# The last experts of a two-layer model: first tiles beside the attention's last batch, gathers queued one part later, sums counted sooner

## The chip, the core and the metric

The kernel runs on one core of one Trainium2 chip. A core has several engines, each with its own queue of instructions that it executes in order: PE (TensorE: matrix products and transposes; its weight loads are shown as PEld), DVE (VectorE), ACT (ScalarE), POOL (GpSimd) and SP (SyncE, which here only issues DMAs). Engines wait for one another by semaphores. Between its inputs and outputs in HBM and the engines lie the on-chip memories SBUF and PSUM; matrix products are written to PSUM. Transfers run on 16 DMA engines.

The metric is the device time of one execution in microseconds (us), as a median of several runs. A profile is one execution taken by the hardware profiler; its span is the time from its first to its last instruction.

## What is computed

Four batches of 1024 rows with 256 columns pass two layers. Each layer has an attention and a feed-forward part with experts, both behind a modulated layer norm. The change touches only the end of the second layer, which the reference computes like this:

```python
def _L1_attn_ref(x, w_qkv, w_proj, b_proj, w_dwc, b_dwc):
    ...
    q = _norm_last(q ** FOCUS)
    k = _norm_last(k ** FOCUS)
    kv = jnp.einsum('bhnd,bhne->bhde', k, v)
    z = 1.0 / (jnp.einsum('bhnd,bhd->bhn', q, k.sum(axis=2)) + EPS)
    out = jnp.einsum('bhnd,bhde,bhn->bhne', q, kv, z)
    ...
    out = out + conv
    return jnp.einsum('bnc,oc->bno', out, w_proj) + b_proj

def _L1_ffn_ref(x, router_w, router_b, expert_w, expert_b):
    ...
    probs = jax.nn.softmax(logits, axis=-1)
    gate = jnp.max(probs, axis=-1)
    idx = jnp.argmax(probs, axis=-1)
    out_all = jnp.einsum('th,ehd->ted', xt, expert_w) + expert_b[None, :, :]
    e_out = jnp.take_along_axis(out_all, idx[:, None, None], axis=1)[:, 0, :]
    y = gate[:, None] * e_out
    ...
    x = x + ga * _L1_attn_ref(h, ...)
    h = _layernorm(x, axis=-1) * (1 + cb) + sb
    x = x + gb * _L1_ffn_ref(h, ...)
```

Every row goes to one of eight experts, the one with the greatest probability; the expert is one product with a 256 x 256 matrix.

## The kernel before

The kernel computes only the chosen expert of a row. So the rows are sorted by expert first, and every tile of 128 sorted rows belongs to one expert.

**The second attention** (`attention1`) goes over the batches with two generators: `front(b)` makes the keys, values and queries of batch b, `back(b - 1)` the output of the batch before. In the last turn of the loop (b = 4) only `back(3)` runs: ps_o (product with kv), its transposes ps_oT, the convolution y (one ACT step at L1597 and two DVE steps at L1601 for each half of the channels) and the projection ps_pr (L1609), which is added to x.

**Around it** runs other work. `k.around` (class `Around`) holds `tasks`, generators that are advanced by so many pieces after each step of the attention, and `riders`, generators of DMAs on POOL's queue, of which one instruction is issued for each "ride". A step has one ride in the attention and two in the last stage. A scatter or a gather also waits for the matmul that was the last to be emitted before it (`paced`, with `k.anchor`). Within what the dependencies allow, the order on an engine is that of a scheduler; `k.pin` keeps an instruction in the order of the program.

**The last experts** (`Experts1`) work in three parts, `PARTS = ((0, 1), (2,), (3,))`: part 0 is batches 0 and 1 (22 tiles, worked on as 11 pairs), parts 1 and 2 are one batch each (14 tiles, 7 pairs). A part goes through these steps:
- `rows(b)`, a task: the statistics of the rows, the normalised rows h (ACT, L1030; first four tiles, later the other four), their store to rows_in, transposes ps_lnT, the router's products ps_route and the logits.
- `sort(p)`, a task: a chain of small DVE operations with three small products (ps_rank, ps_expert) that gives the place of each row (index) and each tile's expert (offset).
- `send(p)`, a rider: POOL loads rows (hs, L1870) and scatters them to their sorted places (L964), 16 scatters for part 0 and 8 for each other part.
- the pairs, in `run`: SP loads a pair of tiles xs (L1008; up to four pairs ahead, and only once the part is sent), PE transposes it (ps_xT, L1923), ACT copies it to xT (L1927, or two scaled copies at L1930 in parts 1 and 2), PE multiplies it with the expert's weights (ps_y, L1938, whose addresses come from registers that each pair loads from offset, L955), DVE adds the bias (L1944) and in parts 1 and 2 multiplies by a gate (L1946), and SP stores the results.
- `combine(p)`, a task: POOL gathers the results in the order of the rows (L974), four tiles ahead of their use with six buffers ys; ACT and DVE scale them and add them to x (L2002, L2007, L2008 in part 0, L1996 in the others), and SP stores the output.

`run` begins when the attention has ended. combine(0) is put among the tasks when the last pair of part 0 is out, so it runs beside part 1's pairs, and combine(1) beside part 2's.

**A check** counts that sums of the attentions lie within bounds (`count_sums`: three times four DVE operations on 512 columns, L495 to L498, at the end of part 1) and branches at the end to a second, general computation, which does not run with these data (`out_of_bounds`).

Of the kernel before, what the change touches and what calls it, by code (L numbers as in the profile page):

```python
# [8 lines left out]
F32 = mybir.dt.float32  # L9
I32 = mybir.dt.int32  # L10
AF = mybir.ActivationFunctionType
# [54 lines left out]
def bcast(ap, axis, n):  # L66

    shape = list(ap.shape)
    shape.insert(axis, n)
    return ap.unsqueeze(axis).to_broadcast(shape)  # L70
# [430 lines left out]
def count_sums(k, pool):  # L501

    recs = [k.recs.rearrange("p n i j -> p (n i j)")]
    recs += [k.recs1[:, i].rearrange("p b t h -> p (b t h)") for i in range(2)]
    inverse = 1.0 / SUM_HI, 1.0 / SUM_LO
    for i, (rec, (low, high)) in enumerate(zip(recs, (inverse, (SUM_LO, SUM_HI), inverse))):
        good = pool.tile([P, 8 * B * H], F32, tag="xs", name="good", bufs=6)
        count_within(k, good, rec, low, high, k.good[:, i : i + 1])


def out_of_bounds(k, pool, psum):
# [505 lines left out]
def routed_rows(k, work, b, statistics, scale, shift, wr, br, ne, logits, scalar):  # L1017
# [31 lines left out]
        return h  # L1049

    h = yield from normalised(0)
    for q in range(2):
        hT = work.tile([P, CC, 512], F32, tag="hT", name="hT", bufs=1)
        for cc in range(CC):
            ps = k.misc.tile([P, 512], F32, tag="m", name="ps_lnT")
            for i in range(4):
                tr = nc.tensor.transpose(  # L1057
                    ps[:, i * P : (i + 1) * P], h[:, i, cc * P : (cc + 1) * P], k.ident
                )
                if i == 0:  # L1060
                    k.pin(tr)
            if scale is None:
                nc.scalar.activation(
                    hT[:, cc], ps, AF.Identity,
                    bias=k.modF[:, cc, b : b + 1], scale=k.modF[:, 2 + cc, b : b + 1],
                )
            else:
                nc.scalar.copy(hT[:, cc], ps)
            if q == 0 and cc == CC - 1:
                h = yield from normalised(1)  # L1070
            else:
                yield 1
        yield from route_logits(k, hT, wr, br, ne, work, logits[:, 4 * q : 4 * q + 4])
# [368 lines left out]

def attention1(ctx, k, a, after_batch=lambda b: None):


    nc = k.nc
# [166 lines left out]
            yield  # L1615

    k.misc = ps_m
    for b in range(B + 1):
        while b == HB and k.awaited in k.around.tasks:
            k.around.step()  # L1620
        todo = ([front(b)] if b < B else []) + ([back(b - 1)] if b else [])
        pace = (6, 8, 6, 6, 12)[b]
        n = 0
        while todo:
            todo = [g for g in todo if next(g, k) is not k]
            n += pace
            k.around.step(n // 6)
            n %= 6
        if b:
            after_batch(b - 1)  # L1630

# [152 lines left out]
class Experts1:  # L1784


    def __init__(self, k, a, out):
# [16 lines left out]
        whole = Sorting(k, rt, E1, 1, NT * len(PARTS[0]))  # L1804
        fewer = whole.of_fewer(rt, NT)
        self.sortings = [whole if len(p) > 1 else fewer for p in PARTS]
        self.sent = set()

    def load_weights(self):
        k, a, nc = self.k, self.a, self.k.nc  # L1810
# [52 lines left out]
    def send(self, p, index):  # L1863
# [16 lines left out]
                yield  # L1880
        self.sent.add(p)

    def run(self, early):

        k = self.k
        nc = k.nc
        work = self.back = self.stack.enter_context(
            k.tc.tile_pool(name="f1_work", bufs=2, reuse_waits="tile")
        )
        ps_x = self.stack.enter_context(  # L1890
            k.tc.tile_pool(name="f1_ps_x", bufs=4, space=PSUM, reuse_waits="tile")
        )
        ps_o = self.stack.enter_context(
            k.tc.tile_pool(name="f1_ps_o", bufs=4, space=PSUM, reuse_waits="tile")
        )
        k.misc = ps_x

        pairs = [
            (p, list(range(g, min(g + 2, s.tiles))))
            for p, s in enumerate(self.sortings)  # L1900
            for g in range(0, s.tiles, 2)
        ]
        coming = []

        def fetch(n):

            for p, tiles in pairs[n + len(coming) : n + 5]:
                if p not in self.sent:
                    break
                xs = work.tile([P, 2, C], F32, tag="xs", name="xs", bufs=6)  # L1910
                k.sorted1[p].load(xs[:, : len(tiles)], tiles)
                coming.append(xs)

        def tiles_of(p, tiles, xs):

            n = len(tiles)
            at = self.sortings[p].offsets(
                self.state[p][1], tiles, [mybir.EngineType.PE, mybir.EngineType.DVE]
            )
            ps = ps_x.tile([P, 2, CC, P], F32, tag="m", name="ps_xT")  # L1920
            for j in range(n):
                for cc in range(CC):
                    nc.tensor.transpose(ps[:, j, cc], xs[:, j, cc * P : (cc + 1) * P], k.ident)  # L1923
            xT = work.tile([P, 2, CC, P], F32, tag="xT", name="xT", bufs=3)
            b = PARTS[p][0] if len(PARTS[p]) == 1 else None
            if b is None:
                nc.scalar.copy(xT[:, :n], ps[:, :n])  # L1927
            else:
                for cc in range(CC):
                    nc.scalar.activation(  # L1930
                        xT[:, :n, cc], ps[:, :n, cc], AF.Identity,
                        bias=k.modF[:, cc, b : b + 1], scale=k.modF[:, 2 + cc, b : b + 1],
                    )
            yield
            po = ps_o.tile([P, 2, C], F32, tag="o", name="ps_y")
            for j in range(n):
                for cc in range(CC):
                    k.anchor = nc.tensor.matmul(  # L1938
                        po[:, j], lhsT=xT[:, j, cc], rhs=self.we[:, cc, bass.ds(at[j], C)],
                        start=cc == 0, stop=cc == CC - 1,  # L1940
                    ).ins
            y = work.tile([P, 2, C], F32, tag="y", name="y", bufs=3)
            for j in range(n):
                nc.vector.tensor_tensor(y[:, j], po[:, j], self.be[:, bass.ds(at[j], C)], ALU.add)  # L1944
            if b is not None:
                nc.vector.tensor_tensor(y[:, :n], y[:, :n], bcast(self.gate[:, b], 1, n), ALU.mult)  # L1946
            nc.sync.dma_start(k.results1[p].part(tiles), y[:, :n])

        again, before = None, None
        for n, (p, tiles) in enumerate(pairs):  # L1950
            if p not in self.sent and before is not None:
                next(before, None)
                before = None
            while p not in self.sent:
                k.around.step(1, 2)
            fetch(n)
            now = tiles_of(p, tiles, coming.pop(0))
            next(now)
            if before is not None:
                next(before, None)  # L1960
            before = now
            if n + 1 == len(pairs) or pairs[n + 1][0] != p:
                next(before, None)
                before = None
                if early and p + 2 == len(PARTS):
                    count_sums(k, work)
                if early and p + 1 == len(PARTS):
                    again = out_of_bounds(k, work, ps_x)
                k.around.tasks.append(self.combine(p))
            k.around.step(2, 2)  # L1970
        k.around.drain()
        self.stack.close()
        return again

    def combine(self, p):
        k, work = self.k, self.back
        nc = k.nc
        index, _, part = self.state[p]
        most = self.sortings[p].nt

        def fetch(n):
            ys = work.tile([P, C], F32, tag="ys", name="ys", bufs=6)
            self.sortings[p].gather(ys, k.results1[p], index[:, 0, n : n + 1])
            return ys

        coming = []
        for n in range(4):
            coming.append(fetch(n))
            yield 0.5
        for n in range(most):  # L1990
            j = n % 2
            b, t = PARTS[p][n // NT], n % NT
            ys = coming.pop(0)
            if len(PARTS[p]) == 1:
                xs = k.x[b][:, t]
                k.pin(nc.vector.scalar_tensor_tensor(  # L1996
# [2 lines left out]
            else:  # L1999
                if j == 0:  # L2000
                    y = work.tile([P, 2, C], F32, tag="out", name="out")
                k.pin(nc.scalar.activation(y[:, j], ys, AF.Identity, scale=part[:, n : n + 1]))  # L2002
            if n + 4 < most:
                coming.append(fetch(n + 4))
            if j == 1 and len(PARTS[p]) > 1:
                xs = k.x[b][:, t - 1 : t + 1]
                nc.vector.tensor_tensor(y, y, bcast(self.gate[:, b], 1, 2), ALU.mult)  # L2007
                nc.vector.tensor_tensor(xs, xs, y, ALU.add)  # L2008
            if t % 4 == 3:
                nc.sync.dma_start(  # L2010
# [7 lines left out]
def two_layers(ctx: ExitStack, tc: tile.TileContext, a: dict, out: bass.AP):  # L2018
# [56 lines left out]
    def stages(first, second, early):  # L2075
# [22 lines left out]
        with ExitStack() as s, tc.using_default_side("right"):  # L2098
            if not early:
                with tc.tile_pool(name="f0_ps_end", bufs=2, space=PSUM, reuse_waits="tile") as k.misc:  # L2100
                    k.around.drain()
            second(s, k, a, *([after_attention1] if early else []))
        if not early:
            experts1.load_weights()
            for b in range(B):
# [81 lines left out]
```

## Time and profile before

| what | value |
|---|---|
| median of 3 runs | 1087.06 us (1085.88, 1089.72, 1087.06) |
| profiled execution, its time | 1087.63 us |
| profiled execution, span | 1085.8 us |
| mean granted PE clock | 0.955 |
| PE busy | 945.7 us (87%), 6072 instructions |
| DVE busy | 620.4 us (57%), 1987 instructions |
| ACT busy | 602.5 us (55%), 959 instructions |
| POOL busy | 336.0 us (31%), 528 instructions |

In the profile a line such as `L1938 PE MATMUL ps_y<-we,xT` names the line of the program, the engine, the operation and the tiles that it writes and reads. What stands in square brackets is the idle time of the engine before the instruction, with the work that ended last before it. "issue" means that the profile shows nothing that the engine waited for. The granted clock is a share of PE's full speed. The busy time of an engine is a mean over stages that have different limits; what a change in one stage does is read from that stage.

### The profile page before, as it was taken

Reading aid. Unit: us, or ns where it says so; the run is one execution under the profiler, and the core shown is the slowest. Engines: PE = TensorE matmul, PEld = TensorE weight load, DVE = VectorE, ACT = ScalarE, POOL = GpSimd, SP = SyncE. Lnnn points to the kernel's source line nnn. Section 1 sums busy time; section 2 is a strip of 40 time slices with the busy share of each in tenths; the row PEclk is TensorE's granted clock in tenths of the full one; section 3 lists DMA queues with packets and bytes.
Section 4 is the critical chain, followed back from the end, with each engine's and each line's share of the span. In section 5 each row is a group of like instructions: output and inputs, shape, how many; then the busy total and the mean of one; then the engine's idle time right before and its main releaser. Section 6 shows DMA issues by size and latency. Waiting matters only on the chain.

```text
span 1085.8 us, 18090 instructions
## 1 busy us (share of the span) xinstructions
PE 945.7 (87%) x6072; PEld 559.8 (52%) x6072; DVE 620.4 (57%) x1987; ACT 602.5 (55%) x959; POOL 336.0 (31%) x528
## 2 busy tenths in 40 slices
PE   4899999999999999889679989986997989858760
PEld 2434434443443434335568878874464656547550
DVE  5822235422465155413676767993899968564572
ACT  0368655765477555775555657766654745523430
POOL 2013211311232234663004615612550100553632
PEclk9999999999999999999899999998999899989875
DMA  6995000100010001552825556624223201458764
GB/s 206 358 346 179 1 1 6 40 1 1 1 64 1 1 30 54 201 215 78 317 88 170 197 177 189 196 75 144 67 65 148 88 2 39 141 170 264 240 205 130
DMA packets 97142, 132.89 MB, mean 122 GB/s; under 512 B 8536, under 2 KB 84216, under 8 KB 96528
## 3 DMA queue, kind: packets, MB, share of 16 engines
q1 hardware_dynamic: 84656, 97.27, 26.9%
q0 software_dynamic: 11776, 33.57, 9.9%
q8 instruction: 52, 0.85, 0.3%
q10 hardware_dynamic: 608, 0.79, 0.3%
q14 instruction: 50, 0.41, 0.1%
HBM read 67.85 MB, written 63.75 MB: 121 GB/s over the span
## 4 chain that ended last, share of the span: by engine, by line
PE 63%; DVE 19%; issue 5%; DMA 5%; ACT 4%; POOL 1%; SPq 1%; DVEq 0%; ACTq 0%; POOLq 0%
PE ps_s L388 13%; PE ps_av L453 12%; PE ps_qk L364 6%; PE ps_y L1312 5%; PE ps_h L1247 4%; PE ps_v L349 3%; PE ps_out L427 3%; PE ps_pr L1609 3%; PE ps_y L1938 3%; PE ps_q L1537 2%; PE ps_k L1511 2%; DVE y L1601 2%; DMA ys<-results,index 2%; PE ps_lnT L1057 1%; DVE st L1258 1%
## 5 line engine op out<-in xcount | busy, mean ns | idle before, releaser
L396 ACT ACTIVATE pT<-ps_s 128x1024 f32<-128x1024 f32 x288 | 279.3, 1022 | 169.7 <-PE ps_s L388 167.2
L399 POOL TENSOR_SCALAR_AFFINE_SELECT pT<-pT 128x256 f32<-128x256 f32 x256 | 104.2, 431 | 328.4 <-ACT pT L396 323.7
L388 PE MATMUL ps_s<-qT,kT 32*128 32x512 f32 (+3 forms) x1536 | 178.8, 523 | 0.1
L453 PE MATMUL ps_av<-pT,v 128*32 128x512 f32 (+3 forms) x1536 | 165.2, 497 | 9.4 <-DVE turned L411 5.6
L964 POOL DMA_INDIRECT sorted<-hs,index x96 | 96.2, 1002 | 144.9 <-PE ps_y L1312 73.0
L974 POOL DMA_INDIRECT ys<-results,index x96 | 102.7, 1070 | 119.0 <-DMA results<-y 43.6
L388 PEld LDWEIGHTS ps_s<-qT,kT 32*128 32x128 f32 x1536 | 74.5, 185 | 95.5 <-issue 72.8
L453 PEld LDWEIGHTS ps_av<-pT,v 128*32 128x32 f32 x1536 | 40.6, 108 | 104.0 <-issue 58.7
L1247 PE MATMUL ps_h<-w,xT 128*128 x352 | 82.1, 386 | 6.5 <-DVE mv L1259 3.8
L1312 PE MATMUL ps_y<-w,act 128*128 x352 | 83.7, 392 | 4.2 <-DVE rs_seed L84 2.8
L411 DVE STREAM_TRANSPOSE turned<-ps_av 128x512 f32<-128x512 f32 x32 | 22.8, 712 | 98.9 <-PE ps_av L453 98.6
L1312 PEld LDWEIGHTS ps_y<-w,act 128*128 128x128 f32 x352 | 67.7, 197 | 14.0 <-ACT act L1295 4.8
L1247 PEld LDWEIGHTS ps_h<-w,xT 128*128 128x128 f32 x352 | 66.2, 193 | 15.9 <-issue 4.2
L1295 ACT ACTIVATE act<-ps_hT,gain 128x128 f32<-128x128 f32 x176 | 63.6, 463 | 16.9 <-PE ps_hT L1286 16.8
L1270 ACT ACTIVATE hid<-hid,nmr,rstd 128x256 f32<-128x256 f32 x88 | 47.5, 603 | 39.4 <-DVE nmr L1263 39.2
L1511 PE MATMUL ps_k<-wqkv,hT 128*128 128x512 f32 x128 | 61.9, 603 | 3.6 <-DMA wqkv<-in_wqkv_dram 2.8
L1938 PE MATMUL ps_y<-we,xT 128*128 x200 | 53.0, 412 | 10.6 <-ACT xT L1930 8.4
L371 DVE COPY qT<-ps_qk 128x512 f32<-128x512 f32 x16 | 11.0, 688 | 81.8 <-PE ps_qk L364 81.8
L103 DVE BATCH_NORM_STATS2 ln_st<-x 128x6 f32<-128x256 f32 x128 | 49.2, 407 | 0.5
L1255 DVE TENSOR_TENSOR hid<-ps_h,b 128x256 f32<-128x256 f32 x88 | 33.9, 415 | 26.6 <-PE ps_h L1247 21.5
L1938 PEld LDWEIGHTS ps_y<-we,xT 128*128 128x128 f32 x200 | 38.2, 204 | 20.1 <-ACT xT L1930 11.6
L374 DVE TENSOR_SCALAR kT<-ps_qk,par 128x512 f32<-128x512 f32 x32 | 22.5, 745 | 37.0 <-PE ps_qk L364 37.0
(223 smaller groups left out, 1499.4 us busy)
## 6 DMA issues: line engine op xcount, KB each, us to landing
xs<-sorted SPq DMA_DIRECT2D x69, 256.0 KB, 3.8
results<-y SPq DMA_DIRECT2D x69, 256.0 KB, 3.0
sorted<-zero SPq DMA_DIRECT2D x2, 6016.0 KB, 20.1
rows_in<-h SPq DMA_DIRECT2D x16, 512.0 KB, 2.9
hs<-rows_in POOLq DMA_DIRECT2D x32, 256.0 KB, 3.5
w<-in_w_dram SPq DMA_DIRECT2D x8, 1024.0 KB, 11.3
x<-in_x_dram SPq DMA_DIRECT2D x4, 1024.0 KB, 6.5
b<-in_b_dram SPq DMA_DIRECT2D x2, 2048.0 KB
```

The lines of the kernel that those rows point to most:

```text
L364: nc.tensor.matmul(ps, lhsT=w[:, cc, g * P : (g + 1) * P], rhs=hT[:, cc, hf * 512 : (hf + 1) * 512], start=cc == 0, stop=cc == CC - 1,)
L388: k.anchor = nc.tensor.matmul(pair[hh // 2][:, hh % 2, c0 : c0 + w], lhsT=kTs[o][rows, kb * P : (kb + 1) * P], rhs=qT[rows, q1 - w : q1], ...
L396: nc.scalar.activation(pT, ps, AF.Exp, scale=1.0 / L**0.5)
L399: nc.gpsimd.affine_select(out=pT[:, :, c0 : c0 + P], in_=pT[:, :, c0 : c0 + P], compare_op=ALU.is_ge, fill=0.0, base=0, pattern=[[0, 2], [ ...
L453: nc.tensor.matmul(po[32 * hh : 32 * hh + 32, 512 - w :], lhsT=vs[b % 2][:, kb, 8 * g + 2 * hh + o, :], rhs=exps[b, g, o, u][hh // 2][:, h ...
L964: i = self.k.nc.gpsimd.indirect_dma_start(out=buffer.ap, out_offset=bass.IndirectOffsetOnAxis(ap=index, axis=0), in_=rows, in_offset=None, ...
L974: self.paced(self.k.nc.gpsimd.indirect_dma_start(out=rows, out_offset=None, in_=buffer.ap, in_offset=bass.IndirectOffsetOnAxis(ap=index, a ...
L1247: mm = nc.tensor.matmul(ph[:, j], lhsT=xTs[i // 2][:, j, cc], rhs=w1[:, cc, bass.ds(at[i + j], C)], start=cc == 0, stop=cc == CC - 1,)
L1295: o = nc.scalar.activation(act[:, j, cc], pt[:, j, cc], AF.Gelu, bias=gain[:, 1, cc, t : t + 1], scale=gain[:, 0, cc, t : t + 1],)
L1312: mm = nc.tensor.matmul(po[:, j], lhsT=acts[i // 2][:, j, cc], rhs=w2[:, cc, bass.ds(at[i + j], C)], start=cc == 0, stop=cc == CC - 1,)
L1511: k.anchor = nc.tensor.matmul(ps, lhsT=hT[:, cc, t * P : (t + 1) * P], rhs=wqkv[:, cc, C:], start=cc == 0, stop=cc == CC - 1,).ins
L1938: k.anchor = nc.tensor.matmul(po[:, j], lhsT=xT[:, j, cc], rhs=self.we[:, cc, bass.ds(at[j], C)], start=cc == 0, stop=cc == CC - 1,).ins
```

## The change

Five things are changed, all in the last 160 us:

1. `attention1` calls a function `fill(turn)` in the last turn of its loop. It is `Experts1.beside`: in turns 6, 7 and 8 it emits two, one and one of part 0's pairs. They use two tiles of the attention's pool (spare) in place of the buffers of `run`, and the attention's PSUM tiles. The code of a pair (`fetch`, `tiles_of`) moves from `run` to methods; the first transpose, the copies xT and the first product of each tile are pinned.
2. In the turns b = 3 and b = 4 of the attention a step has two rides.
3. Where the rows are not scaled (batches 2 and 3), `routed_rows` normalises all eight tiles before the first transposes.
4. The gathers become riders (`gathers(p)`), queued when the last pair of a part is out, with 24 buffers ys. combine(0) becomes a task at the end of part 1's pairs, combine(1) and combine(2) after all pairs. A step in `run` has four pieces until the last part is sent.
5. `count_sums` becomes a generator; one of its three counts is emitted after each of the pairs 7, 8 and 9 of part 0, and its tile good gets another tag. `out_of_bounds` comes after all pairs.

```diff
 def count_sums(k, pool):
...
-        good = pool.tile([P, 8 * B * H], F32, tag="xs", name="good", bufs=6)
+        good = pool.tile([P, 8 * B * H], F32, tag="out", name="good")
         count_within(k, good, rec, low, high, k.good[:, i : i + 1])
+        yield
...
     h = yield from normalised(0)
+    second = (yield from normalised(1)) if scale is None else None
...
             if q == 0 and cc == CC - 1:
-                h = yield from normalised(1)
+                if second is None:
+                    h = yield from normalised(1)
+                else:
+                    h = second
+                    yield 1
...
+    k.bank = lambda name: ps_p.tile([P, 2, C], F32, tag="p", name=name)
+    k.spare = lambda: work.tile([P, CC, N], F32, tag="hT", name="spare")
     for b in range(B + 1):
...
             n += pace
-            k.around.step(n // 6)
+            k.around.step(n // 6, 1 + b // (B - 1))
             n %= 6
+            turn += 1
+            if b == B:
+                fill(turn)
...
+    def pair(self):
+
+        self.fetch()
+        p, tiles = self.pairs[self.done]
+        self.done += 1
+        now = self.tiles_of(p, tiles, self.coming.pop(0))
+        next(now)
+        self.products()
+        self.before = now
+        if self.done == len(self.pairs) or self.pairs[self.done][0] != p:
+            self.products()
...
+    def beside(self, turn):
+
+
+        if 0 not in self.sent or turn > 8:
+            return
+        if self.space is None:
...
+            self.space, self.most = space, 4
+        self.fetch()
+        for _ in range({6: 2, 7: 1, 8: 1}.get(turn, 0)):
+            self.pair()
+        if turn == 8:
+            self.products()
...
+        counts = count_sums(k, work) if early else iter(())
+        last = len(PARTS) - 1
+        while self.done < len(self.pairs):
+            p = self.pairs[self.done][0]
+            if p not in self.sent:
+                self.products()
             while p not in self.sent:
-                k.around.step(1, 2)
...
+                around.step(1, 2)
+            self.pair()
+            if p == 0 and self.done > 6:
+                next(counts, None)
+            if self.done == len(self.pairs) or self.pairs[self.done][0] != p:
+                around.riders.append(self.gathers(p))
+                if p == last - 1:
+                    around.tasks.append(self.combine(0))
+            around.step(2 if last in self.sent else 4, 2)
+        for _ in counts:
+            pass
+        again = out_of_bounds(k, work, ps_x) if early else None
+        while around.riders:
+            around.step(0)
+        around.tasks += [self.combine(p) for p in range(1, last + 1)]
+        around.drain()
...
+    def gathers(self, p):
+
+        index = self.state[p][0]
+        for n in range(self.sortings[p].nt):
+            ys = self.back.tile([P, C], F32, tag="ys", name="ys", bufs=24)
+            self.sortings[p].gather(ys, self.k.results1[p], index[:, 0, n : n + 1])
+            self.got[p].append(ys)
+            yield
...
-            ys = coming.pop(0)
+            while not self.got[p]:
+                k.around.step(0)
+            ys = self.got[p].pop(0)
...
-            second(s, k, a, *([after_attention1] if early else []))
+            second(s, k, a, *([after_attention1, experts1.beside] if early else []))
```

## The prediction

> **What bounds the kernel now.** The change touches only the last 160 us, so I read those. First the busy time of each engine in six stretches (from:to, length, then busy us and instructions of PE, weight loads, DVE, ACT and POOL, the granted PE clock, DMA share, GB/s):
>
> ```profile
> core 0: us, PE busy (x) PEld busy (x) DVE busy (x) ACT busy (x) POOL busy (x), PEclk, DMA share, GB/s
> 945.20:960.50 15.30, 5.98 (x56) 4.83 (x56) 12.46 (x45) 6.03 (x10) 8.50 (x10) 0.78 0.47 151
> 960.50:969.50 9.00, 9.00 (x36) 7.58 (x35) 4.56 (x15) 0.00 (x0) 2.08 (x2) 0.80 0.68 219
> 969.50:1006.40 36.90, 31.57 (x198) 24.76 (x197) 17.17 (x74) 13.96 (x26) 16.80 (x19) 1.00 0.80 253
> 1006.40:1033.50 27.10, 19.20 (x82) 15.13 (x82) 15.49 (x30) 13.13 (x29) 17.71 (x17) 0.87 0.72 224
> 1033.50:1062.20 28.70, 18.97 (x78) 14.77 (x78) 22.68 (x51) 7.24 (x15) 8.47 (x8) 0.82 0.66 209
> 1062.20:1085.80 23.60, 0.00 (x0) 0.00 (x0) 3.79 (x9) 0.00 (x0) 8.07 (x8) 0.52 0.39 118
> ```
>
> The first two are the end of the second attention (convolution on ACT and DVE, then the projection ps_pr). The third holds part 0's eleven pairs of tiles and, between them, the routing and sorting of the last batch. The fourth is part 1, the fifth part 2, the sixth the last gathers and stores. In no stretch after 969.5 but the third is PE near full, so the pairs wait for something. The timeline (start, length) says for what, with the wait in square brackets:
>
> ```profile
> 956.56 0.97 POOL L964 DMA_INDIRECT sorted<-hs,index  x1 [0.30 <-issue]
> 959.07 11.75 SPq L1008 DMA_DIRECT2D xs<-sorted  x8
> 960.40 0.20 PE L949 MATMUL ps_expert<-past,all 8*1 8x14 f32 x2 [7.67 <-DVE index L933]
> 960.54 8.94 PE L1609 MATMUL ps_pr<-wg,y 128*128 128x256 f32 x32
> 1019.01 3.54 PE L1938 MATMUL ps_y<-we,xT 128*128 x8 [3.58 <-ACT xT L1930]
> 1048.90 2.30 PE L1923 MATMUL ps_xT<-ident,xs 128*128 128x128 f32 x8 [6.42 <-DMA xs<-sorted]
> 1061.46 0.69 DVE L1946 TENSOR_TENSOR y<-y,gate_f 128x512 f32<-128x512 f32 x1
> 1065.12 1.00 POOL L974 DMA_INDIRECT ys<-results,index  x1 [14.78 <-DMA results<-y]
> ```
>
> Three marks carry the sum: ps_pr ends at 960.54 + 8.94 = 969.48 (T); the first ps_y of part 1 starts at 1006.40 (S); the span ends at 1085.8, 79.4 after S. The waits from 1006.4 to 1062.2 (total, times, longest):
>
> ```profile
> ACT out L2002 <- DMA ys<-results,index: 10.6, 8, 2.6
> PE ps_y L1938 <- ACT xT L1930: 8.4, 4, 3.6
> PE ps_xT L1923 <- DMA xs<-sorted: 6.4, 1, 6.4
> ```
>
> ACT waits in its own order for a gathered tile, and the scaled copies xT stand behind it, so PE waits for ACT; later PE waits for a load of xs that stands on SP behind stores of results.
>
> **Part by part.** *Two riders a step.* From its first scatter at 927.17 POOL issues a scatter every 1.31 us and an hs load every 1.06 (the rows of L964 and L1870). In the built order 4 hs loads stand between the 16 scatters: 15 x 1.31 + 4 x 1.06 = 23.9, so the last starts at 951.1 and not 956.56: 5.5 earlier. The loads of xs follow 2.5 later (956.56 to 959.07) and land in 3.8 to 4.1: the first tile is there at 957.6 (L). If the scatters keep the waits that they have now for buffers (1.74 and 2.10 on POOL), L is nearer 960; if the loads had landed as fast as the results do (3.0), 956.6. I take 957.6, as the waits came where one rider a step held the queue.
>
> *First pairs beside the attention.* The built order on PE is what matters. The first ps_xT of a pair, which waits for all 16 scatters and the load, now stands before the rest of the last batch: three ps_o tiles, the second lnT and route of batch 2, the eight ps_oT, logits, rank, then four pairs' ps_y, ps_expert, ps_pr. Before, ps_xT stood behind ps_pr. So from about 945.5 PE does nothing until L, some 12 us, and the attention waits with it. After L:
> - the work that ran from 945.24 to 951.08 (5.8 us), mostly still to do, 5.5; at half clock for its first 3.6 us, 1.8 more: ps_oT ends at L + 7.3;
> - from ps_oT to ps_pr it took 951.08 to 960.54 = 9.5 (ACT y, then four DVE steps L1601 of 1.20). Now ACT has two copies xT between its two y (2 x 0.59), and DVE has four bias adds (0.42 and 0.34) and two to four register loads of 0.53 (the median of L955 on DVE's queue) between those steps: 1.2 + 1.5 + 1.1 to 2.1, so 3.8 to 4.8; the last step also stands behind pair 1's y, some 1 more. PE's four pairs (8 transposes of two pairs 1.04, 8 records of ps_y 1.99: 2.5 each, 10.1) fit beside that. ps_pr starts at L + 21.5 to 24; I take 22.5;
> - ps_pr without the half clock: 1.3 less than 8.94, 7.6.
>
> T becomes 957.6 + 22.5 + 7.6 = 987.7: **18.2 later**.
>
> *T to S.* Four pairs fewer stand here, 10.1 us of PE. They buy little: the stretch is a chain from ps_pr over statistics (mv at T + 4.2), normalise, transposes, route, logits (T + 18.9), the sort (index at T + 26), ps_expert, then pairs 7 to 10, counted from 0 (y from 997.41) and S. The built order still puts ps_y of pairs 7 to 10 behind ps_expert. The second normalise goes ahead, but ACT does all eight in a row before the first hT copy, so one gains what the other loses; the logits come about 0.5 earlier. Two of the counts of sums (0.42 + 0.42 + 0.68 + 0.68 by L495 to L498) now stand among the sort's small DVE steps: 0.5 to 1.5. Taken: 37.4 for 36.9, **0.5 later**; from 5 earlier (PE's idle 36.9 - 31.57 = 5.3, if it was PE that held the chain) to 1.5 later.
>
> *S to the end.* Gathers are queued on POOL one part later into 24 buffers and no ACT or DVE instruction waits for them in part 1: pairs at the rate of the undisturbed ones (ps_y at 1006.40 and 1008.70, 2.2 with the next), 7 x 2.2 = 15.4. Part 2's first load of xs is queued on SP ahead of part 1's stores of results, so the wait of 6.42 goes; but it waits for part 2's scatters, behind which those stores stand: hidden as long as it lands before S + 15.4 (last scatter about S + 3, landing about 7 more), else its lateness is added. In part 2 combine(0) runs beside the pairs, and DVE sets the rate: 7 x (0.67 + 0.6) for y and gate, 8 x (0.6 + 0.6) for out and x, 7 x 0.53 of register loads: 22.2. Then the tail as now, 1085.8 - 1062.15 = 23.65 (the gathers of part 2 wait for all its results, as before; combine(1) lies in their wait of some 3 + 10.5 us). S to end: 15.4 + 22.2 + 23.65 = 61.2 instead of 79.4: **18.2 earlier**, 14 to 20 by part 2 at 2.8 (before's 1056 to 1062) or with one more half clock stretch.
>
> Sum against the profiled run: +18.2 + 0.5 - 18.2 = +0.5; span 1086.3, and with 1.8 around it (1087.63 - 1085.8) 1088.1. The profiled run lies 0.6 above the median of 1087.06, so this is +0.5 on like terms; I keep 1088.5.
>
> The half clock speaks against this change. The rows show what idling PE costs:
>
> ```profile
> 960.40:964.00 3.60, 3.60 (x10) 2.92 (x11) 0.21 (x2) 0.00 (x0) 0.00 (x0) 0.50 0.96 294
> 1048.90:1056.10 7.20, 6.81 (x21) 5.22 (x22) 2.23 (x6) 2.04 (x4) 1.22 (x1) 0.50 0.67 234
> ```
>
> After 7.7 idle the clock is 0.50 for 3.6 us, after 6.4 idle for 7.2. The new stall of 12 us invites either: 1.8 (taken) or 3.6.
>
> The Trainium skill, "TensorE: Matmul & The Clock Gate", section "What's actually happening", has the clock fall to half after an idle window of about 3.4 us and come back after as long a busy one. The first row agrees, the second stays down twice as long; by the page the price would be 1.7 and the time 1088, by the second row 3.6 and 1090, and its advice to avoid such gaps speaks against putting a waiting transpose ahead of ready work.
>
> **Rivals.** *The chain from T to S was held by PE.* For it: PE is busy 31.57 of 36.9 there. Against it: the logits wait for ACT's h and hT, and rank for DVE. If so S comes 5.3 sooner, and the full gain behind S (20) adds 1.8: 1088.1 - 7.1 = 1081. *The first load is late.* The attention now waits for POOL's last scatter. Each us that L is late is a us of the end. For it: POOL's scatters now wait for buffers (1.74 and 2.10); with these and a lag as today's the load lands at 959.07 + 3.9 = 963, 5.4 later: 1093.5, and with the clock down 7.2 us 1095.3. It decides from L = 960 (1090.3 is 2.2 above the sum). Against it: nothing else stands on POOL then. *The riders and early pairs are hidden anyway* would give the 18.2 without the stall, 1070; the built order speaks against it, since ps_oT can't pass ps_xT on PE.
>
> **How the numbers follow.** Gain and stall cancel: 0.42, own range 1083 to 1094. PE held the chain (or a shorter stall): 0.28, 1072 to 1083. The first load late (or a slower part 2): 0.30, 1091 to 1102. The predicted time is the first's, 1088.5. A measurement of this kernel can tell 0.3% (3.3 us) from no change, so same is 1083.8 to 1090.3. Of the first case 0.04 lies below it, 0.24 in it, 0.14 above: faster 0.32, same 0.24, slower 0.44. For 8 in 10 the range runs from 1077 to 1101.
>
> **What would show it.** PE idle from about 945 to L near 957.6, ended by a DMA into spare, with ps_oT behind it; ps_pr ending at 987 to 989; 36 to 38.5 from there to part 1's first ps_y; no wait of ACT for ys before part 2; part 2's pairs 2.9 to 3.2 apart with DVE nearly full; the tail near 23.6. Wrong if the stall is under 8 us or over 16, if the early pairs shorten T to S by over 2, or if part 1 waits for its stores behind part 2's loads.

## The result and the profile after

The changed kernel took 1096.3 us (median of 5 runs, 1093.42 to 1098.08) against 1087.06 (5 runs): a ratio of 1.0081, with a 95% interval of 1.0057 to 1.0105. It is slower, by 0.8%. Its profiled execution has a span of 1095.9 us, 10.1 more than before.

The busy time by stages after the change (the columns are those of before):

```profile
core 0: us, PE busy (x) PEld busy (x) DVE busy (x) ACT busy (x) POOL busy (x), PEclk, DMA share, GB/s
946.60:961.47 14.87, 0.77 (x9) 0.54 (x5) 0.68 (x2) 0.62 (x1) 8.12 (x9) 0.59 0.49 153
961.47:989.60 28.13, 25.85 (x142) 21.58 (x143) 18.84 (x65) 7.19 (x11) 6.45 (x7) 0.85 0.43 140
989.60:1029.02 39.42, 27.55 (x152) 21.69 (x149) 20.63 (x81) 11.91 (x22) 12.86 (x15) 0.83 0.57 188
1029.02:1044.50 15.48, 15.23 (x82) 13.14 (x82) 7.71 (x16) 7.80 (x17) 9.73 (x11) 1.00 0.79 257
1044.50:1070.30 25.80, 16.33 (x78) 11.94 (x78) 22.06 (x43) 12.00 (x27) 16.75 (x16) 0.97 0.85 265
1070.30:1095.90 25.60, 0.00 (x0) 0.00 (x0) 8.26 (x19) 0.00 (x0) 8.22 (x8) 0.50 0.51 162
```

The first row is new: for 14.9 us four engines do next to nothing and only POOL works. The fourth row is the gain: part 1 on a PE that is full, 15.5 us where part 1 took 27.1. The third row took 36.9 before and has fewer pairs in it now, but a lower clock. The timeline after:

```profile
954.03 0.98 POOL L965 DMA_INDIRECT sorted<-hs,index  x1 [0.31 <-issue]
...
956.60 1.90 SPq L1009 DMA_DIRECT2D spare<-sorted  x4
...
961.47 0.48 PE L1921 MATMUL ps_xT<-ident,spare 128*128 128x128 f32 x1 [14.10 <-DMA spare<-sorted]
...
968.61 1.09 PE L1595 MATMUL ps_oT<-ident,on 128*128 128x128 f32 x8
...
982.43 7.17 PE L1615 MATMUL ps_pr<-wg,y 128*128 128x256 f32 x32
...
994.58 0.47 PE L1059 MATMUL ps_lnT<-ident,h 128*128 128x128 f32 x1 [4.54 <-ACT h L1031]
...
1074.98 1.00 POOL L975 DMA_INDIRECT ys<-results,index  x1 [9.16 <-DMA out_dram<-x]
```

PE waits 14.1 us for the first early pair's load. The last ps_o tiles and the second half of ps_oT, which PE had done by 951.1 in the kernel before, come after it. The marks of the prediction give this balance. "Start" is the first scatter of part 0, which is ahead of the stages compared here; what lies before it was 2.3 us longer in this execution. That difference is there long before anything that the change touches: ps_expert of the first layer starts at 573.92 instead of 571.98. In all fourteen profiles of this document that mark lies between 569.2 and 575.1, so 2.3 is no more than executions differ there.

| stretch | before | after | difference | predicted |
|---|---|---|---|---|
| up to the start | 927.2 | 929.4 | +2.3 | 0 |
| start to the end of ps_pr (T) | 42.3 | 60.2 | +17.9 | +18.2 |
| T to part 1's first ps_y (S) | 36.9 | 39.4 | +2.5 | +0.5 |
| S to the last gate of part 2 | 55.75 | 41.3 | -14.45 | -18.2 for both |
| last gate to the end | 23.65 | 25.6 | +1.9 | |
| span | 1085.8 | 1095.9 | +10.1 | +0.5 |

So the large loss came as worked out, and the gain behind S was 12.5 us and not 18.2.

### The profile page after: what moved, and what is told of

Its sections match the earlier page's. It is cut to its first block, busy times and chain, and to the rows that moved or that the text cites. A ratio compares the mean times of both kernels' runs of the same rounds, so it can differ in the third digit from the quotient of the medians.

```text
span 1095.9 us, 18076 instructions
## 1 busy us (share of the span) xinstructions
PE 949.6 (87%) x6072; PEld 564.2 (51%) x6072; DVE 622.3 (57%) x1987; ACT 602.2 (55%) x959; POOL 335.4 (31%) x528
## 5 line engine op out<-in xcount | busy, mean ns | idle before, releaser
L453 PEld LDWEIGHTS ps_av<-pT,v 128*32 128x32 f32 x1536 | 40.8, 109 | 102.9 <-issue 59.7
L411 DVE STREAM_TRANSPOSE turned<-ps_av 128x512 f32<-128x512 f32 x32 | 22.8, 712 | 97.9 <-PE ps_av L453 97.6
L1276 ACT ACTIVATE hid<-hid,nmr,rstd 128x256 f32<-128x256 f32 x88 | 47.5, 603 | 39.9 <-DVE nmr L1269 39.8
L1938 PE MATMUL ps_y<-we,xT 128*128 x168 | 44.1, 408 | 3.0 <-ACT xT L1930 2.8
L374 DVE TENSOR_SCALAR kT<-ps_qk,par 128x512 f32<-128x512 f32 x32 | 22.5, 746 | 37.7 <-PE ps_qk L364 37.7
L1327 DVE TENSOR_TENSOR y<-ps_y,b 128x256 f32<-128x256 f32 x88 | 35.1, 418 | 15.0 <-PE ps_y L1318 14.8
```

Source lines behind the costliest of these rows:

```text
L453: nc.tensor.matmul(po[32 * hh : 32 * hh + 32, 512 - w :], lhsT=vs[b % 2][:, kb, 8 * g + 2 * hh + o, :], rhs=exps[b, g, o, u][hh // 2][:, h ...
L1276: o = nc.scalar.activation(h[:, i], h[:, i], AF.Identity, bias=nmr[:, i : i + 1], scale=rstd[:, i : i + 1])
```

## The experiments

Runs of one group were taken on one chip, and every ratio is against the kernel before on that chip. The chips differ: before took 1098.4 us on the chip of the first group, 1087.1 on that of the second, 1098.9 on that of the third. Marks are compared within a group, or, across groups, only as lengths from the start. A ratio is not quite the quotient of the two medians of a group (for g4 1.0099 and 1.0129).

### First group: no early pairs, other rows, counts late

e1 leaves the early pairs out (e2 to e4 build on it or on the changed kernel):

```diff
-            second(s, k, a, *([after_attention1, experts1.beside] if early else []))
+            second(s, k, a, *([after_attention1] if early else []))
```

> The changed kernel with fill left out: no pair beside the attention, all else as changed. Theory A (the transposes that wait for the first xs hold the whole end of the attention, and the four early pairs return nothing): ps_pr ends about 17.9 us earlier than in the changed kernel; but the step of four pieces lets the sort end after three pairs, so eight pairs stand behind ps_expert instead of four, and 4 x 2.2 = 8.8 us are added from there to part 1's first ps_y. Time 1096.3 - 17.9 + 8.8 = 1087. Rival B (the stall only covers waits that the attention has anyway, and the early pairs are worth their 10.1 us of PE): the time rises, 1100 or more.

e2 adds two pieces a step:

```diff
-            around.step(2 if last in self.sent else 4, 2)
+            around.step(2, 2)
```

> As e1, with two pieces a step in place of four while part 0 is worked on, as before the change, so that pairs and the last batch's sort are mixed as before. Theory A: the end of ps_pr as in e1, from there to part 1's first ps_y 36.9 as before instead of 39.4, from there to the end 66.9 as in the changed kernel: 1096.3 - 17.9 - 2.5 = 1076, which would beat both kernels. Rival B: 1098 or more. Rival C (what is gained behind part 1's first ps_y needs the early pairs or the four pieces): 1087, as before.

e3 is the changed kernel with another source for the early pairs:

```diff
-            self.k.sorted1[p].load(xs[:, : len(tiles)], tiles)
+            from_ = self.k.rows_in[0] if self.most == 4 else self.k.sorted1[p]
+            from_.load(xs[:, : len(tiles)], tiles)
```

> The changed kernel, but the four early pairs read rows of rows_in, which are long there, and not the sorted rows: that part of the computation is changed. The pairs stay beside the attention, and only their wait for the scatters is gone. Theory A: the stall of 14.1 us before the first ps_xT goes and with it the half clock behind it (up to 1.8): 1096.3 - 14.1 to 15.9, so 1080 to 1082. Rival B (the stall is cover for the convolution's own waits): 1091 or more.

e4 is e2 with the counts where they were:

```diff
-            if p == 0 and self.done > 6:
-                next(counts, None)
...
                 if p == last - 1:
+                    for _ in counts:
+                        pass
                     around.tasks.append(self.combine(0))
```

> As e2, with the three counts of sums at the end of part 1, as before the change. Theory A: DVE sets the rate in part 2, so the 3 x 2.2 = 6.6 us of counts that come to stand there are paid, less what was idle there (3.7 of 25.8 us): 3 to 6 above e2, about 1080. Rival (the counts are hidden beside part 2's loads): within 1.5 of e2.

| run | ratio, 95% interval | start to T | T to S | S to end |
|---|---|---|---|---|
| e1 | 1.0105 (1.0051 to 1.0159) | 45.9 | 47.5 | 76.3 |
| e2 | 1.0016 (0.9985 to 1.0047) | 45.4 | 45.2 | 72.6 |
| e3 | 0.9994 (0.9965 to 1.0023) | 47.1 | 41.2 | 73.4 |
| e4 | 1.0027 (0.9992 to 1.0062) | 45.9 | 45.5 | 74.2 |

e3 answers the first question. The timeline of e3:

```profile
946.30 0.60 PE L1922 MATMUL ps_xT<-ident,spare 128*128 128x128 f32 x4
...
975.24 7.17 PE L1615 MATMUL ps_pr<-wg,y 128*128 128x256 f32 x32
...
1042.59 1.02 ACT L1931 ACTIVATE xT<-ps_xT,modF 128x256 f32<-128x256 f32 x2 [7.53 <-remote]
```

With rows that were there long before, the first early transpose runs 11 us after the start instead of 32, and T comes 13.0 sooner after the start than in the changed kernel (47.1 to 60.2). Against before, 4.8 are left (47.1 to 42.3); the pairs' own work is at most 1.7 of them, as e2 and e4, which have no early pairs, also stand at 45.4 and 45.9. So the wait, and not the pairs' work, is the main loss. The time fell by 0.9% (1.0081 to 0.9994), some 9 us where 14 to 16 were expected. The third line shows part of the rest: ACT stood for 7.5 us at the last pair of part 1 for something that the profile calls remote, that is, a wait whose end it can put down to no engine and no transfer of this core.

e1 and e2 missed my expectation: without the early pairs the time was not 1076 but that of before. T did come back to 45.4 to 45.9 after the start (in e1 with remote waits of 4.3 and 4.8 on ACT and DVE that end at 957.8), but T to S was 45 to 47.5 and not 37. The traces show why: with four pieces a step (e1) the sort ends after three pairs, and eight stand behind ps_expert; with two (e2) it ends after six, and five stand behind it, where four did before. e4 settled little: its T to S is e2's, its interval overlaps e2's. In e2 ACT stands 9.0 us and DVE 4.1 us for remote in the stages behind S, so S to the end is no clean figure there; e4 has none of it there, and its 74.2 holds the counts.

### Second group: the two kernels again, the second normalise, gathers and counts alone

> The changed kernel, unaltered, on the same chip as the next three, for marks that can be compared with theirs. Theory A: about 1.008 of before, PE idle some 14 us before the first early transpose. Rival: the 0.8% came from the chip or the hour, then 1.000 to 1.004 here.

> The kernel before, unaltered, for its trace on this chip. Expected: a ratio of 1.000 within the interval; from the first scatter of part 0 to the end of ps_pr 42.3, from there to part 1's first ps_y 36.9, from there to the end 79.4, each plus whatever this chip adds.

f3 undoes part 3 of the change:

```diff
-    second = (yield from normalised(1)) if scale is None else None
+    second = None
```

> The changed kernel with part 3 of the change undone: the second four tiles of batches 2 and 3 are normalised when they were before. Theory A (as predicted: one gains what the other loses): within 1.5 us of the changed kernel. Rival: eight normalises in a row on ACT (4.0 us) push the first copies hT and with them the route and the attention's end; then undoing it gives 2 to 4 us.

f4 is e2 with that line and with one ride a step again:

```diff
-            k.around.step(n // 6, 1 + b // (B - 1))
+            k.around.step(n // 6)
```

> Only parts 4 and 5 of the change (gathers one part later into 24 buffers, combine(0) beside part 2, counts sooner), with two pieces a step; no early pairs, one ride in the attention, second normalise as before. Theory A: end of ps_pr as before, to part 1's first ps_y 37 to 40 (five pairs instead of four stand behind ps_expert), from there to the end 67 as in the changed kernel instead of 79.4: 9 to 12 us faster than before, a ratio of 0.989 to 0.992. Rival (the shorter time behind part 1's first ps_y in the changed kernel was bought by what came earlier: four pairs and their results were already out): from there to the end 73 to 76, ratio 0.996 to 1.002.

| run | ratio, 95% interval | start to T | T to S | S to end |
|---|---|---|---|---|
| f1, changed | 1.0070 (1.0045 to 1.0095) | 58.5 | 39.9 | 66.7 |
| f2, before | 1.0000 (0.9979 to 1.0020) | 42.2 | 37.5 | 78.9 |
| f3 | 1.0067 (1.0047 to 1.0088) | 55.6 | 40.3 | 67.1 |
| f4 | 0.9951 (0.9931 to 0.9971) | 42.2 | 46.1 | 65.8 |

f1 and f2 repeat the result, stretch by stretch (+16.3, +2.4, -12.2). The time of f3 is that of the changed kernel, so no worth of the second normalise is shown either way, though in f3's one profile T comes 2.9 sooner after the start. f4 is faster than before by 0.5% (by the medians 6.4 us): the gathers and counts, with the pins, bring the whole gain behind S (65.8 for 78.9), so it was not bought by the early pairs. But f4 loses 8.6 of it between T and S. The stages of f4 (T to S, part 1), and T to S of f2:

```profile
967.24:1013.35 46.11, 35.19 (x199) 28.02 (x197) 23.59 (x87) 15.01 (x28) 16.79 (x19) 0.89 0.66 209
1013.35:1028.70 15.35, 15.15 (x84) 13.19 (x82) 9.15 (x18) 6.75 (x15) 9.69 (x9) 1.00 0.88 267
```

```profile
966.98:1004.44 37.46, 31.60 (x199) 24.81 (x197) 17.17 (x74) 13.95 (x26) 16.78 (x19) 1.00 0.78 250
```

The same 199 matmuls in 46.1 us instead of 37.5, at a clock of 0.89 instead of 1.00. Two lines of f4's timeline show where:

```profile
995.92 0.67 DVE L498 TENSOR_REDUCE good<-good 128x1 f32<-128x512 f32 x1
...
997.18 0.20 PE L950 MATMUL ps_expert<-past,all 8*1 8x14 f32 x2 [3.96 <-DVE past L946]
```

A count of sums stands on DVE right before the operation that ps_expert waits for, PE idles 4.0 us, and five pairs stand behind ps_expert where four did. Counted from T, ps_expert starts 3.0 later than in f2 (at 29.95, there at 26.96), and the stretch from there to S takes 16.2 for 10.5. In the changed kernel's code the pairs' first transpose, the copies and the first product of each tile are pinned to the order of the program, which before they were not.

### Third group: pins, counts, combine(0), and the early pairs once more

g1 takes the pins away from f4:

```diff
-                if j == cc == 0:
-                    k.pin(tr)
...
-            k.pin(nc.scalar.copy(xT[:, :n], ps[:, :n]))
+            nc.scalar.copy(xT[:, :n], ps[:, :n])
```

(and the same for the scaled copies and the products)

> f4 (gathers and counts only) with the pairs' transposes, copies and products not pinned to the order of the program, as before the change. The built order then has four pairs and not five behind ps_expert. Theory A (in f4 the pins hold ps_expert back and leave pairs behind it, 46.1 instead of 37.5 from the end of ps_pr to part 1's first ps_y): 37.5 to 40 there, 65.8 from there to the end: 6 to 8 us less than f4, ratio 0.988 to 0.990. Rival (the counts among the sort's DVE steps do it): as f4, 0.994 to 0.996.

g2 moves the counts to part 1:

```diff
-            if p == 0 and self.done > 6:
+            if p == last - 1 and self.done > 12:
```

> As g1, and the three counts beside part 1's pairs (DVE is busy for half of that stage) instead of among the last sort's steps. Theory A: 1 to 2.5 less than g1, ratio 0.986 to 0.989. Rival (the counts were hidden): as g1 within 1.

g3 starts combine(0) sooner:

```diff
-                if p == last - 1:
-                    around.tasks.append(self.combine(0))
+            if self.done == 15:
+                around.tasks.append(self.combine(0))
```

> As g2, and combine(0) begins after the fourth pair of part 1, not after the seventh. In the changed kernel part 2's pairs are 3.6 apart with DVE 22.1 of 25.8 busy, part 1's 2.2 with DVE half idle. Theory A (DVE sets part 2's rate): some 4 of combine(0)'s 8 groups at 1.4 move to part 1, 3 to 5 us less than g2, ratio 0.982 to 0.985. Rival (then ACT waits for gathered tiles in part 1 again, as before the change): not faster than g2.

g4 is g2 with the two rides and with `experts1.beside` again.

> g2 with the four early pairs and the two rides added: the first two parts of the change alone, on the best ground. The first early transpose still stands ahead of three ps_o tiles and the second ps_oT on PE. Theory A: ps_pr ends 13 to 16 later, and with four pairs fewer between it and part 1 at most 9 come back: 4 us or more above g2, ratio 0.991 or more. Rival (the early pairs are worth their PE time once the rest is in order): g2 or less.

| run | ratio, 95% interval | start to T | T to S | S to end |
|---|---|---|---|---|
| g1 | 0.9967 (0.9943 to 0.9992) | 42.7 | 40.8 | 73.3 |
| g2 | 0.9913 (0.9879 to 0.9947) | 42.9 | 40.9 | 72.2 |
| g3 | 0.9901 (0.9873 to 0.9929) | 44.0 | 41.8 | 66.6 |
| g4 | 1.0099 (1.0062 to 1.0136) | 58.3 | 29.7 | 86.9 |

Without the pins T to S is 40.8 instead of 46.1, a little above the 37.5 to 40 that were expected: four pairs stand behind ps_expert again and take 11.9, while a count still stands ahead of it (28.9 after T). The ratio of g1, though, is no better than f4's, which was taken on another chip; in g1's profile ACT and DVE stand again for remote between S and the end:

```profile
DVE y L1943 <- remote: 8.9, 2, 6.1
ACT xT L1928 <- remote: 8.4, 1, 8.4
```

The counts in part 1 (g2) bring 0.5% by the ratios, 0.4% by the medians, with intervals that just meet. That is more than the 1 to 2.5 us expected, and the two profiles don't show it: their spans are 1094.6 and 1094.2, and g2's profiled execution is the slowest of its four. In g2 ps_expert does come sooner, 27.1 after T, but behind it ACT stands 5.6 us and DVE 4.3 us for remote, and g3's T to S holds such waits too (4.9 and 3.7). That g3 is faster than g2 is not shown (0.9901 and 0.9913). Both beat the kernel before: g3 is 1.0% faster (0.7 to 1.3; 0.8% by the medians). The lines of its parts 1 and 2, and g2's:

```profile
1025.70:1041.00 15.30, 12.95 (x66) 10.65 (x66) 12.27 (x27) 6.45 (x14) 9.35 (x8) 1.00 0.76 228
1041.00:1067.60 26.60, 18.67 (x94) 14.52 (x94) 22.49 (x47) 13.35 (x30) 19.09 (x17) 1.00 0.90 282
```

```profile
1022.00:1037.30 15.30, 15.23 (x82) 13.15 (x82) 12.05 (x27) 7.24 (x15) 8.88 (x8) 1.00 0.85 264
1037.30:1068.60 31.30, 18.02 (x78) 13.77 (x78) 22.60 (x46) 12.73 (x28) 18.03 (x17) 0.89 0.69 214
```

In both DVE has 22.5 to 22.6 of work in the second stretch; g3's is 4.7 shorter, but g2's holds an ACT wait of 8.0 for remote. So DVE is busy for most of g3's part 2 (22.5 of 26.6), and the worth of the earlier start is not shown.

g4 shows the early pairs on their best ground, and one more trap. T comes 15.4 later than in g2 and T to S is 11.2 shorter, a loss of 4.2 by the pairs; it is rough, as ACT has remote waits around T in g4 and behind ps_expert in g2. All seven pairs that are left stand ahead of ps_expert here, and none behind it. The rest of its loss is a new wait:

```profile
1050.24 1.02 POOL L965 DMA_INDIRECT sorted<-hs,index  x1 [0.30 <-issue]
...
1064.99 1.08 PE L1921 MATMUL ps_xT<-ident,xs 128*128 128x128 f32 x4 [24.91 <-DMA xs<-sorted]
```

Riders go in the order in which they were queued. With two pieces a step, part 0's pairs are out before the last sort is, so part 0's 16 gathers are queued on POOL ahead of part 2's scatters, and PE waits 24.9 us for part 2. In the changed kernel the scatters end at 1031 and the gathers begin at 1033; by the code it is the four pieces a step that keep this order, which was not tried alone.

## Why the prediction came out as it did

*The stall.* Right, in place and size. Predicted: the last scatter 23.9 after the first, the load there at 957.6, which is 30.4 after the start, T 18.2 later. Measured: 24.6, 32.0, 17.9. The load was 1.6 late: SP issued 2.6 behind the last scatter, as predicted, but the landing took about 4.9 and not 3.8 to 4.1. From there to ps_pr it took 21.0 for 22.5, and ps_pr took 7.2 for 7.6. So the agreement within 0.3 is in part luck: the load was late by about as much as the work behind it was quick. Two slips of the working are small beside that: the 1.8 that the prediction takes for a half clock would put ps_pr at 7.1 and not 7.6, and +0.5 on the median is 1087.6 and not the 1088.5 that was kept. e3 shows that the wait is the cause: with the pairs in place and the wait gone, T comes 13.0 sooner.

*T to S.* As predicted, four pairs fewer there bought nothing; it took 2.5 longer and not 0.5. Counted from T, the logits are there at 18.9 (19.1 before), ps_expert starts at 27.5 (26.4) and S comes at 39.4 (36.9). The first two are close to the prediction, which had the logits 0.5 sooner and then 0.5 to 1.5 for the counts. The step that failed is the last one: the sum has no term for the four pairs behind ps_expert, and they took 11.9 for 10.5, at a lower clock. The same stretch, from ps_expert to S, before and after:

```profile
995.90:1006.40 10.50, 10.36 (x60) 8.87 (x61) 3.70 (x12) 2.96 (x6) 7.87 (x8) 1.00 0.90 291
```

```profile
1017.09:1029.02 11.93, 11.08 (x57) 9.53 (x57) 6.52 (x17) 2.38 (x5) 6.85 (x7) 0.86 0.61 203
```

g1 has the same four pairs at the same clock, 11.9 at 0.86. PE idles 4.5 us before 994.58, and again 2.5 and 1.9 around the sort; before, the clock was 1.00 from T to S. The clock in two stretches after:

```profile
994.50:1000.10 5.60, 5.41 (x16) 4.11 (x17) 0.00 (x0) 4.72 (x10) 0.00 (x0) 0.50 0.52 151
1010.70:1022.10 11.40, 8.64 (x35) 7.34 (x36) 5.97 (x28) 1.17 (x2) 2.09 (x3) 0.70 0.28 92
```

The first of them cost the chain nothing, as the logits came no later than before; the second covers the first pair behind ps_expert, and the later pairs ran as before. f4, without the early pairs, loses clock there too (0.89), with the pins and a count ahead of ps_expert; the pins stood in the diff and the prediction gave them no price at all.

Which pairs moved explains why they bought nothing. Before, seven pairs stand between T and ps_expert and four behind it; in the changed kernel it is three and four. What left was work in the time in which the sort is awaited anyway, and e1 and e2 show that the four pieces a step make that order. In g4, with two pieces and no pins, it is seven and none, and T to S is 29.7.

The Trainium skill, "TensorE: Matmul & The Clock Gate", section "What's actually happening", gives an idle window of some 3.4 us before the clock falls and a busy one as long before it returns, and says that these windows run freely, whenever the work starts. The row from 994.50 agrees with the fall (4.5 idle). The clock stayed at 0.50 for 5.6 us of it with PE busy for 5.4; that agrees with the return only if the work began inside a window, for which an estimate from the page's figure allows up to 6.8.

*S to the end.* Part 1 was right on PE (15.5 for 15.4, and ACT waits for no gathered tile there). Two terms were mis-sized. Part 2 took 25.8 for 22.2, with DVE the busiest engine, as predicted (22.06 busy). The groups from S on:

```profile
L1947 DVE TENSOR_TENSOR y<-ps_y,be 128x256 f32<-128x256 f32 x28 | 10.9, 418 | 8.9 <-DMA results<-y 3.6 <-issue 2.9 <-PE ps_y L1938 2.2
L1949 DVE TENSOR_TENSOR y<-y,gate_f 128x512 f32<-128x512 f32 x14 | 9.7, 692 | 0.4
...
L2070 DVE TENSOR_TENSOR x<-x,out 128x512 f32<-128x512 f32 x8 | 5.6, 694 | 0.3
L2069 DVE TENSOR_TENSOR out<-out,gate_f 128x512 f32<-128x512 f32 x8 | 5.5, 694 | 2.0 <-ACT xT L1930 1.3 <-issue 0.6
```

Two things made that work larger. I had counted each operation on 512 columns at 0.6. An operation that follows one whose result it does not read does start 0.61 to 0.66 after it here, but one that reads it starts 0.72 to 0.76 after it, as the gates and the adds to x do:

```profile
1048.14 0.68 DVE L2069 TENSOR_TENSOR out<-out,gate_f 128x512 f32<-128x512 f32 x1
1048.86 0.69 DVE L2070 TENSOR_TENSOR x<-x,out 128x512 f32<-128x512 f32 x1
1049.52 0.69 DVE L2069 TENSOR_TENSOR out<-out,gate_f 128x512 f32<-128x512 f32 x1
```

And DVE was behind PE: when PE began part 2's products at 1044.5, the adds and gates of two of part 1's pairs were still to do, so that the stretch held nine pairs, and seven of combine(0)'s eight groups. With 0.69 an operation and 0.76 for two bias adds that is 9 x 1.45 + 7 x 1.39 = 22.8, near the 22.06 busy. The prediction's 7 x 1.27 + 8 x 1.2 = 18.5 was 3.6 too small, which is the whole difference. The tail took 25.6 for 23.65. The chain of waits after:

```profile
1070.35 3.69 DMA results<-y
...
1084.33 2.95 DMA ys<-results,index
```

The last store of results took 3.7 us to land where it took 2.17 before; behind it the first gather starts 4.7 after the last gate, and 3.0 before. combine(0) now runs to the last pair, so its out_dram stores go out beside that store; the timeline even puts the gather's wait down to one of them. That this is the cause is likely and was not tried alone: the gather starts 4.5 to 5.4 after the last gate in the profiles where combine(0) runs so late, and 3.9 in g3, where it has ended before the last gate.

*The rivals.* That PE held the chain from T to S was not what the changed kernel showed, as T to S grew. It is not refuted as such: in g4, where no pair is left behind ps_expert, T to S falls by 11.2 against g2, more than the rival's 5.3. That the first load is late came true by 1.6 us only, and quicker work behind it took that back. What made the time rise over the sum is 2.0 between T and S, 5.7 behind S, and 2.3 that lie ahead of all that was changed. The likeliest case, gain and stall cancel, was therefore not what happened. The time lay 7.8 above the predicted 1088.5, in the wide range from 1077 to 1101, and in the third case's part of it (a late load or a slower part 2); of these two it was mainly part 2.

**What stays open.** What remote means. The name ends waits of up to 8.4 us on ACT and DVE behind S, and some ahead of it, in profiles of the first and the third group, and occurs in none of the six profiles of the two kernels and of the second group. In the window of e3's 7.5 us the trace also shows a transfer of instructions; but the changed kernel's profile has such transfers in part 1 too, and no such wait. What the gain behind S is on the chips of the first and the third group can't be told, as no profile of before was taken there. Early pairs with a source that does not wait, with the right rows and with the order of riders kept, were not built.

## What to carry to other kernels

An engine that works in order stops for the first instruction that is not ready, with all that stands behind it: before work is put "beside" other work, look at which instruction of it comes first in the engine's built order and what that one waits for. A change of several parts is worth taking apart: here two of five parts held the whole gain, 0.5% with the pins and 1.0% in g3, which leaves the order of the pairs free, puts the counts in part 1 and starts combine(0) sooner. Which of the three makes the difference is not shown, as the two were measured on two chips. Taking work away pays only where it stood on the chain: look at which of it stood behind the step that everything waits for. Durations for a sum come from rows where the operations depend on each other as they will, not from overlapping neighbours.

## What the runs showed of the hardware

After 4.5 us of idling PE ran at a granted clock of 0.50 for 5.6 us, with 5.4 of work in them. The same four pairs took 10.5 us at a clock of 1.00 and 11.9 at 0.86, in two builds. On DVE an operation on 512 columns starts 0.72 to 0.76 us after one whose result it reads, and 0.61 to 0.66 after another. And the kernel before took 1087.06, 1087.1, 1098.4 and 1098.9 us in four groups of runs, the last three on three chips: a spread of 1.1%, more than most parts of the change are worth, so only ratios taken on one chip could tell them apart.
